# An end stage re-balanced: crossed halves evicted by ScalarE, two stores a chunk, a sixth image convolved again, two more buffers

## The chip, the cores and the metric

The kernel runs on one core of one Trainium2 chip. The core has TensorE (PE, matrix products), ScalarE (ACT), VectorE (DVE), GpSimd (POOL) and SyncE (SP); SP issues nearly all loads and the stores to scratch, POOL the stores of the result. 16 DMA engines move the data. The metric is the device time in microseconds (us).

## The reference

The input x is 16 images of 64 channels and 128 x 128 pixels, fp32. Four residual layers follow one another, each on a group norm of x (32 groups of 2 channels):

```
x = x + conv1x1(gram(gn(x)) @ gn(x))                  # layer 0
x = x + |sobel_x(gn(x))| + |sobel_y(gn(x))|           # layer 1
x = x + conv3x3(temporal_shift(gn(x)), W) + b         # layer 2
y = conv1x1(conv3x3(gn(x), w_bin), w1x1) + b1x1       # layer 3
y = batch_norm(y) over all 16 images                  # mean and variance per channel
x = x + clip(leaky(y), 0, 255)
```

The batch norm needs the sums of y over every pixel of every image before a single result can be finished. So layer 3 has a first pass, which makes y and its sums, and an end stage, which normalizes, clips, adds and writes the result.

## The kernel before, in words

**Main pipeline.** An image is cut into NS = 8 chunks of 2 x 8 rows: partitions 0 to 63 hold 64 channels of the upper half of the image, partitions 64 to 127 those of the lower half. A loop over steps (lines 1176 to 1242) lets three stages, Front (layers 0 and 1), Layer2 and Layer3, work on different images in the same step; `starts` (line 1091) holds their offsets. Every instruction goes through `InOrder`, so each engine runs its instructions in the order in which the Python code emits them. Layer 2 writes its result, the input of layer 3, to a scratch tensor `x3_d` (`put_rows`, line 817), layer 3 its y to `y_d` (line 1059). In the profile both the layer-1 and the layer-2 scratch tensors are called `x_d`.

**Two kinds of images.** For images in `AGAIN` (line 24: 3, 4, 5, 6, 7), y is summed but not stored (line 1059), their x3 is stored in upper and lower halves (`in_halves`, line 819) and their norm coefficients are kept (line 894). In the end stage their chunks are *convolved again*: x3 is loaded, normed, and convolved with the combined weights. For the other images y and x3 are only *loaded*.

**The end stage's list.** Lines 1113 to 1121 write out the order: `todo` holds an entry "again" for every chunk of an image in AGAIN, and an entry "loaded" for every eighth of another image. It starts with two "again" and eight "loaded" (`ahead`), ends with six "loaded" (`behind`), and spreads the others evenly between the "again" entries.

**Buffers and loads.** `room` is a queue of free buffers of 128 x 1024 fp32 (0.5 MB). `fetch` (line 1146) takes the next entry of `todo`, takes one buffer ("again") or two ("loaded") from the front of `room` and issues the loads on SP. Buffers are what the main pipeline no longer needs: from line 1212 on pieces of xw and xh and the tiles x, xr, u and e, at the last image v2, d2[1], q2 and x3, and after the loop (lines 1245 and 1246) the last x3 and y. Loads are issued in the last steps already, as far as room goes. In the end loop `fetch` runs while more than 8 buffers lie in `room` (line 1355).

**The end loop** (lines 1335 to 1358). For "again": `again_close` lets ACT norm the row below the chunk that came before, and `again_products` emits that chunk's matmuls. For "loaded": ACT takes a relu with the batch norm's scale and shift in place, DVE clips and adds, POOL stores 0.5 MB; then `again_out` finishes the chunk convolved before the newest one, and `again_in` lets ACT norm the newest chunk into `v_again`. `again_products` (line 1299) works on 64 x 64 quarters of the array: output row groups g = 0, 1 and input halves h = 0, 1 give four products at a time into `two_again`, whose group g = 0 has the halves in place and whose group g = 1 has them crossed: half h lies in the partitions of half 1 - h. So the residual rows of g = 1 are moved across too, by two products with the identity into `rest_again`, in PSUM. `again_out` (line 1319) then evicts each group by one ACT instruction into z, DVE clips and adds, and POOL stores each group's two halves: four stores of 128 KB a chunk.

The tiles `two` (tag "two") and the v3 tiles have two buffers each, z has one per group.

Of the kernel before, what the change touches and what calls it, by code (L numbers as in the profile page):

```python
# [10 lines left out]
F32 = mybir.dt.float32  # L11
AF = mybir.ActivationFunctionType
ALU = mybir.AluOpType
AX = mybir.AxisListType

B, C, H, W = 16, 64, 128, 128
P = 128
# [3 lines left out]
R = 8  # L21
NS = HH // R
EARLY = 3
AGAIN = (3, 4, 5, 6, 7)
CP = 4
GN_EPS = 1e-5
BN_EPS = 1e-5
# [83 lines left out]
def tile_kernel(ctx: ExitStack, tc: tile.TileContext, x, cw_h, w2_t, b2, wbin_t, w1_t, b1, gamma, beta, consts, out):  # L111
    nc = tc.nc
    pe, dve, act, sp, pool = (InOrder(tc, e) for e in (nc.tensor, nc.vector, nc.scalar, nc.sync, nc.gpsimd))
# [8 lines left out]
    def k(name):  # L122
        return kc[:, AT[name][0]:AT[name][1]]

    def const(shape, name):
        return cpool.tile(shape, F32, name=name)
# [3 lines left out]
    gamma_sb, beta_sb = (const([P, 2], n) for n in ("gamma_sb", "beta_sb"))  # L130
    kept = const([P, len(AGAIN), 2], "kept")
    bn_sum = cpool.tile([P, B * NS], F32, name="bn_sum")
# [7 lines left out]
    def flat(ap):  # L140
        return ap.rearrange("p j w -> p (j w)")

    def halves(d, h, r0, n):

        v = d[0:C * HW].rearrange("(c r) -> c r", r=HW)
        return v[:, (h * HH + r0) * W:(h * HH + r0 + n) * W]
# [15 lines left out]
    ps_one = ctx.enter_context(tc.tile_pool(name="ps_one", bufs=1, space=PSUM))  # L162
    ps_po = ctx.enter_context(tc.tile_pool(name="ps_po", bufs=1, space=PSUM))
# [6 lines left out]
    def cols(o):  # L170
        return slice(o * C, (o + 1) * C)
# [53 lines left out]
    d2, q2, d3 = [], None, None  # L225
    for name in ("d2a", "d2b", "q2", "d3"):
        t = wpool.tile([P, 2, CP, W + 2], F32, name=name)
# [5 lines left out]
        else:  # L233
            d3 = t
# [319 lines left out]
    lo, hi = slice(0, C), slice(C, P)  # L554
# [262 lines left out]
    def put_rows(b, s, j, t):  # L817

        in_halves = b in AGAIN
        size = NP // 2 if in_halves else NP  # L820
# [15 lines left out]
    class Layer2:  # L836
# [49 lines left out]
        def done(self, co):  # L886
# [5 lines left out]
            coefs3[self.b] = co, edge  # L892
            if self.b in AGAIN:
                pool.tensor_copy(kept[:, AGAIN.index(self.b)], co[:, 0:2])

# [101 lines left out]
    class Layer3:  # L997
# [34 lines left out]
        def at(self, i, q):  # L1032
# [10 lines left out]
            if q == 1:  # L1043
# [13 lines left out]
                if 1 <= i:  # L1057
                    y = self.y.pop(i - 1)
                    for s in range(0 if b in AGAIN else 2):
                        for z in range(2):  # L1060
# [42 lines left out]
    at = 12  # L1103
# [8 lines left out]
    N = R * W  # L1112
    parts = deque((b, q) for b in range(B) if b not in AGAIN for q in range(C * HW // P // N))
    again = deque((b, i) for b in AGAIN for i in range(NS))
# [19 lines left out]
    def rest(pool, tag, shape, bufs, n=None):  # L1134
        for m in range(bufs if n is None else n):
            t = pool.tile([P] + shape, F32, tag=tag, name=f"end_{tag}_{len(room)}", bufs=bufs)
            while len(t.shape) > 2:
                t = t.rearrange("p a b c -> p (a b) c" if len(t.shape) == 4 else "p a b -> p (a b)")
            room.append(t[:, 0:N])

    def slices(t, n):
        room.extend(t[:, j * N:(j + 1) * N] for j in range(n))
# [3 lines left out]
    def fetch():  # L1146
        n = fetched[0]
        if n == len(todo):
            return 2
        way, b, q = todo[n]  # L1150
        if way == "loaded":
            yt, rt = room.popleft(), room.popleft()
            sp.dma_start(yt, whole(y_d[b], q))
            sp.dma_start(rt, whole(x3_d[b], q))
            loaded.append((yt, rt))
        else:
            t = room.popleft()
            sp.dma_start(t, x3_d[b].rearrange("(p n) -> p n", p=P)[:, q * N:(q + 1) * N])
            loaded.append((t,))
        fetched[0] += 1  # L1160
        return len(loaded[-1])
# [14 lines left out]
    for step in range(starts[2][1] - 2, steps):  # L1176
        now[0] = step
        for q in range(4):
            for b in range(B):

                i = step - starts[2][1] - NS * b
# [11 lines left out]
            for b in range(1, B):  # L1193
                at, n = pace[b]
# [28 lines left out]
            if step >= last_one and q == 2:  # L1223

                n = 3 if step == last_one else 1 if step < last_one + NS - 2 else 0
# [13 lines left out]
            if step >= last_one - NS and q == 3:  # L1239
                n = 0  # L1240
# [3 lines left out]
        tick()  # L1244
    rest(ring, "x3", [2, CP, W], NS + 2, NS + 2 - 3 - (NS - 3))
    rest(ring, "y", [2, CP, W], 2)
    while len(room) > 1 and fetched[0] < len(todo):
        fetch()

# [12 lines left out]
    def pair(name):  # L1262
        return cpool.tile([P, 2], F32, name=name)
# [13 lines left out]
    sc = pair("sc")  # L1277
# [5 lines left out]
    shb = cpool.tile([P, 1], F32, name="shb")  # L1283
# [15 lines left out]
    def again_products():  # L1299

        v, r, b, i = at_hand[-1]
        two = ps_two.tile([P, 2, CP, W], F32, tag="two", name=f"two_again_{b}_{i}")
        pool_, tag = ((ps_po, "po"), (ps_one, "one"))[(b * NS + i) % 2]
        rest_ = pool_.tile([P, CP, W], F32, tag=tag, name=f"rest_again_{b}_{i}")
        for h in range(2):
            pe.matmul(rest_[cols(1 - h)], k("I")[cols(h), cols(h)], r[cols(h), CP:R, :], start=True, stop=True)
        order = [(ky, kx) for kx in (1, 0, 2) for ky in range(3)]
        for n, (ky, kx) in enumerate(order):
            o0, o1 = (0, W) if kx == 1 else (1, W) if kx == 0 else (0, W - 1)
            for g in range(2):  # L1310
                for h in range(2):
                    j = g * CP + ky
                    pe.matmul(
                        two[cols(h if g == 0 else 1 - h), g, :, o0:o1], rows_of[ky, h][:, kx],
                        v[cols(h), j:j + CP, o0 + kx - 1:o1 + kx - 1], start=n == 0, stop=n + 1 == len(order),
                    )
        summed.append((two, rest_, r, b, i))

    def again_out():

        two, rest_, r, b, i = summed.popleft()
        to = out[b].rearrange("c h w -> (c h w)")
        for g, (tag, add) in enumerate((("c2", r[:, 0:CP, :]), ("c3", rest_))):
            z = ring.tile([P, CP * W], F32, tag=tag, name=f"z_{b}_{i}_{g}", bufs=1)
            act.activation(z, flat(two[:, g]), AF.Relu, bias=shb, scale=sc[:, 1:2])
            to_rows = flat(r[:, g * CP:(g + 1) * CP, :])
            dve.scalar_tensor_tensor(to_rows, z, 255.0, flat(add), op0=ALU.min, op1=ALU.add)
            for h in range(2):
                pool.dma_start(halves(to, h if g == 0 else 1 - h, i * R + g * CP, CP), to_rows[cols(h)])
        room.append(flat(r))  # L1330

    rows_of = {(kk, i): w3[cols(i), slot, :, cols(o)] for slot, i, o, kk in TO_PAIRS}
    summed, coming = deque(), deque()

    for n, (way, b, q) in enumerate(todo):
        if way == "again":
            (t,) = loaded.popleft()
            if n > 0:
                again_close(t)
                again_products()  # L1340
                coming.append((b, q, t))
        else:
            yt, rt = loaded.popleft()
            act.activation(yt, yt, AF.Relu, bias=sh[:, 0:1], scale=sc[:, 0:1])
            dve.scalar_tensor_tensor(rt, yt, 255.0, rt, op0=ALU.min, op1=ALU.add)
            pool.dma_start(whole(out[b].rearrange("c h w -> (c h w)"), q), rt)
            room.extend((yt, rt))
            if len(summed) > 1 or summed and n > len(todo) - behind + 1:
                again_out()
            if coming:  # L1350
                again_in(*coming.popleft())
            elif n == len(todo) - behind + 1:
                again_close(None)
                again_products()
        while len(room) > 8 and fetched[0] < len(todo):
            fetch()
    while summed:
        again_out()
# [38 lines left out]
```

## Time and profile before

| | |
|---|---|
| median of 3 runs | 2587.8 us (2585.97 to 2590.42) |
| the profiled execution | 2585.35 us, its span 2583.5 us |
| PE busy over the span | 2421.9 us (94%) |
| DVE, ACT busy | 2086.3 (81%), 2075.6 (80%) |
| POOL busy | 539.8 (21%) |
| moved by DMA | 613.29 MB, 237 GB/s on the mean |

The stages, from the busy times by stage:

| window, us | what | PE busy | DVE | ACT | POOL | GB/s |
|---|---|---|---|---|---|---|
| 200 to 2111 | the pipeline, three stages at once | 1874.83 | 1752.65 | 1657.59 | 344.27 | 205 |
| 2111 to 2174 | layer 3 of the last image alone | 59.59 | 20.75 | 48.40 | 0.00 | 220 |
| 2174 to 2583.5 | the end stage | 359.53 | 158.95 | 241.28 | 132.94 | 403 |

A busy time is the sum of an engine's instructions, overlap counted once. GB/s is what all DMA engines moved in the window. A line in order of time begins with start and length in us, then names engine, operation, and the tile written and the tile read. "SPq" is SP's queue of DMA issues; its length is the time that the issues span, not the transfer. Two 64 x 64 matmuls that run side by side are recorded each, and an fp32 matmul is recorded twice, so the 36 products of a chunk convolved again are 72 records (2880 for 40 chunks).

### The profile page before, as it was taken

What the parts mean: (1) busy time and instruction counts of PE and PEld (TensorE: products, weight loads), DVE (VectorE), ACT (ScalarE), POOL (GpSimd) and SP (SyncE); (2) the same over time, 40 slices, a digit from 0 to 9 for tenths busy, and PEclk for the clock granted to TensorE, in tenths of its full rate; (3) what the DMA queues carried; (4) which work ended last, traced back from release to release, by engine and by line L of the source; (5) the groups of instructions that cost most, each with busy time, mean ns of one, the idle gap of its engine ahead of it and who ended that gap; (6) DMA issues with size and microseconds to landing.
All of it is one profiled execution on the core that took longest, in us unless ns stands there. A gap on an engine that the chain in (4) does not pass through costs nothing.

```text
span 2583.5 us, 52173 instructions
## 1 busy us (share of the span) xinstructions
PE 2421.9 (94%) x18790; PEld 959.1 (37%) x18790; DVE 2086.3 (81%) x2803; ACT 2075.6 (80%) x3467; POOL 539.8 (21%) x876
## 2 busy tenths in 40 slices
PE   6568899999999999999999999999999999999885
PEld 4334343434343434343434343333333333333332
DVE  4998899999999999999999999999996334433333
ACT  4778879898989898989898988888987668655554
POOL 3332312111121212111212121202110101333332
PEclk8679999999999999999999999999999999999998
DMA  8789979898977777777778877877876877999998
GB/s 200 200 231 241 241 178 251 213 247 208 241 190 201 188 193 190 197 193 187 200 199 222 226 191 192 206 198 203 212 194 170 199 208 252 415 417 417 416 415 354
DMA packets 635809, 613.29 MB, mean 237 GB/s; under 512 B 55280, under 2 KB 535312, under 8 KB 635552
## 3 DMA queue, kind: packets, MB, share of 16 engines
q1 hardware_dynamic: 601376, 505.08, 71.2%
q0 software_dynamic: 34176, 104.88, 12.2%
q8 instruction: 149, 2.44, 0.4%
q14 instruction: 108, 0.88, 0.1%
HBM read 325.59 MB, written 247.47 MB: 222 GB/s over the span
## 4 chain that ended last, share of the span: by engine, by line
PE 48%; DMA 19%; DVE 13%; ACT 8%; issue 5%; SPq 5%; POOL 1%; DVEq 0%; POOLq 0%; ACTq 0%
PE two L74 24%; PE one L74 16%; SPq L74 5%; DVE u L74 5%; PE bank L74 3%; PE po L74 3%; DMA xw<-y_d 3%; DVE e L74 2%; DMA x_d<-u 2%; DMA end_x<-x_d 2%; ACT v L74 2%; DMA xw<-x_d 2%; DVE d L74 2%; DMA v<-x_d 2%; DVE y L74 1%
## 5 line engine op out<-in xcount | busy, mean ns | idle before, releaser
L74 PE MATMUL two<-d,w 64*64 64x512 f32 (+2 forms) x2992 | 692.5, 593 | 0.0
L74 PE MATMUL two_again<-v_again,w 64*64 64x508 f32 (+1 forms) x2880 | 357.0, 598 | 20.9 <-ACT v_again L74 20.8
L74 PE MATMUL one<-v,w 128*64 128x508 f32 (+2 forms) x1600 | 358.8, 580 | 8.1 <-ACT c L74 7.8
L74 PEld LDWEIGHTS two<-d,w 64*64 64x64 f32 (+1 forms) x2992 | 206.6, 134 | 418.0 <-issue 408.1
L74 PE MATMUL one<-v,wi 128*64 128x508 f32 (+3 forms) x1536 | 352.5, 593 | 0.0
L74 DVE SCALAR_TENSOR_TENSOR e<-e 128x1032 f32<-128x1032 f32 (+1 forms) x256 | 313.2, 1224 | 0.0
L74 ACT ACTIVATE xh<-po,co 128x128 f32<-128x128 f32 (+1 forms) x480 | 274.5, 621 | 25.5 <-PE po L74 20.5
L74 PE MATMUL po<-x,abd 64*64 64x512 f32 (+1 forms) x1024 | 187.1, 623 | 53.4 <-ACT xh L74 50.0
L74 DVE SCALAR_TENSOR_TENSOR y<-two,c 128x1024 f32<-128x1024 f32 x128 | 156.1, 1220 | 92.5 <-ACT v L74 62.3
L74 POOL DMA_DIRECT2D q<-d2b x138 | 72.1, 527 | 720.5 <-DVE d2b L74 409.7
L74 PE MATMUL two<-q,cross 64*64 64x508 f32 (+3 forms) x944 | 216.6, 573 | 0.0
L74 PEld LDWEIGHTS two_again<-v_again,w 64*64 64x64 f32 x2880 | 135.6, 134 | 211.5 <-issue 169.7
L74 POOL DMA_DIRECT2D q<-d2a x138 | 73.7, 537 | 641.1 <-issue 284.0
L74 ACT ACTIVATE v<-x,co 128x1024 f32<-128x1024 f32 (+3 forms) x256 | 203.8, 847 | 0.0
L74 DVE TENSOR_TENSOR d<-v 128x1024 f32<-128x1024 f32 x128 | 156.2, 1220 | 47.0 <-ACT v L74 29.3
L74 PEld LDWEIGHTS one<-v,w 128*64 128x64 f32 x1600 | 110.0, 136 | 202.8 <-issue 160.5
L74 ACT ACTIVATE v<-v,co 128x1154 f32<-128x1154 f32 x128 | 172.1, 1345 | 16.1 <-DMA x_d<-x 6.6
L74 PE MATMUL two<-d2a,wi 128*64 128x508 f32 (+1 forms) x768 | 183.2, 589 | 0.0
L74 DVE SCALAR_TENSOR_TENSOR u<-xh 128x1170 f32<-128x1170 f32 x128 | 175.9, 1374 | 5.9 <-ACT xh L74 4.7
L74 DVE SCALAR_TENSOR_TENSOR u<-xh,co,u 128x1024 f32<-128x1024 f32 x128 | 163.8, 1280 | 15.7 <-ACT u L74 15.6
L74 PE MATMUL two<-d2b,wi 128*64 128x508 f32 (+3 forms) x768 | 175.2, 567 | 0.0
L74 PEld LDWEIGHTS one<-v,wi 128*64 128x64 f32 x1536 | 101.1, 138 | 193.8 <-issue 154.9
(265 smaller groups left out, 4349.8 us busy)
## 6 DMA issues: line engine op xcount, KB each, us to landing
x<-in_x SPq DMA_DIRECT2D x256, 256.0 KB
x_d<-u SPq DMA_DIRECT2D x512, 128.0 KB
x_d<-x SPq DMA_DIRECT2D x491, 128.0 KB
xr<-in_x SPq DMA_DIRECT2D x120, 512.0 KB
y_d<-y SPq DMA_DIRECT2D x352, 128.0 KB
v<-x_d SPq DMA_DIRECT2D x448, 72.1 KB
v<-x_d SPq DMA_DIRECT2D x224, 144.2 KB
end_x<-x_d SPq DMA_DIRECT2D x42, 512.0 KB
```

Of the source, the lines that this page charges most:

```text
L74: return self.tc.keep_in_program_order(call(*args, **kwargs))
```

## The change

Four edits. (1) `rest_again` and its products with the identity go; ACT's eviction of the crossed group is split into two instructions of 64 partitions, each reading one half of `two_again` and writing the other half of z, so z has its halves in place and DVE adds the residual from the loaded tile. (2) POOL stores each half of a finished chunk, both groups at once: two stores of 256 KB in place of four of 128 KB. (3) Image 8 joins `AGAIN`, so 48 chunks are convolved again and 80 parts are loaded, in place of 40 and 88; its y is not stored in the first pass. (4) After the loop, d2[0] and d3, tiles of layer 3, join `room`, behind the last x3 and y tiles.

```
-AGAIN = (3, 4, 5, 6, 7)
+AGAIN = (3, 4, 5, 6, 7, 8)
...
     rest(ring, "y", [2, CP, W], 2)
+    for t in (d2[0], d3):
+        slices(t.rearrange("p n j w -> p (n j w)"), 1)
     while len(room) > 1 and fetched[0] < len(todo):
         fetch()
...
         two = ps_two.tile([P, 2, CP, W], F32, tag="two", name=f"two_again_{b}_{i}")
-        pool_, tag = ((ps_po, "po"), (ps_one, "one"))[(b * NS + i) % 2]
-        rest_ = pool_.tile([P, CP, W], F32, tag=tag, name=f"rest_again_{b}_{i}")
-        for h in range(2):
-            pe.matmul(rest_[cols(1 - h)], k("I")[cols(h), cols(h)], r[cols(h), CP:R, :], start=True, stop=True)
...
-        summed.append((two, rest_, r, b, i))
+        summed.append((two, r, b, i))
...
-        two, rest_, r, b, i = summed.popleft()
+        two, r, b, i = summed.popleft()
         to = out[b].rearrange("c h w -> (c h w)")
-        for g, (tag, add) in enumerate((("c2", r[:, 0:CP, :]), ("c3", rest_))):
+        for g, tag in enumerate(("c2", "c3")):
             z = ring.tile([P, CP * W], F32, tag=tag, name=f"z_{b}_{i}_{g}", bufs=1)
-            act.activation(z, flat(two[:, g]), AF.Relu, bias=shb, scale=sc[:, 1:2])
+            for o, at in ((slice(0, P), slice(0, P)),) if g == 0 else ((lo, hi), (hi, lo)):
+                act.activation(z[o], flat(two[at, g]), AF.Relu, bias=shb[at], scale=sc[at, 1:2])
             to_rows = flat(r[:, g * CP:(g + 1) * CP, :])
-            dve.scalar_tensor_tensor(to_rows, z, 255.0, flat(add), op0=ALU.min, op1=ALU.add)
-            for h in range(2):
-                pool.dma_start(halves(to, h if g == 0 else 1 - h, i * R + g * CP, CP), to_rows[cols(h)])
+            dve.scalar_tensor_tensor(to_rows, z, 255.0, to_rows, op0=ALU.min, op1=ALU.add)
+        for h in range(2):
+            pool.dma_start(halves(to, h, i * R, R), flat(r)[cols(h)])
         room.append(flat(r))
```

## The prediction

> **What bounds the kernel now.** I read the page's slices first, then busy time by stage, then the chain of waits, and last the order of instructions on TensorE (PE), ScalarE (ACT) and SyncE's queue (SP) inside the last stage. Busy time by stage (columns: window, length, then busy us of PE, weight loads, VectorE (DVE), ACT, GpSimd (POOL), granted clock, DMA share, GB/s):
>
> ```profile
> 2176.00:2186.00 10.00, 10.00 (x86) 3.52 (x80) 7.39 (x11) 9.29 (x9) 2.67 (x5) 0.87 0.94 322
> 2240.00:2290.00 50.00, 50.00 (x448) 19.77 (x442) 19.68 (x21) 29.76 (x37) 18.26 (x34) 1.00 1.03 417
> 2340.00:2550.00 210.00, 188.06 (x1590) 72.35 (x1584) 75.45 (x83) 121.15 (x150) 65.55 (x123) 1.00 1.03 416
> ```
>
> The DMA engines move 416 to 417 GB/s in both later windows, so they are full from about 2186 us. PE is full too in the second window, but not in the third. The chain of waits agrees: through the stage it goes from load to load down to 2500 us, such as (start, us)
>
> ```profile
> 2198.12 19.30 DMA end_x<-x_d
> 2217.49 19.93 DMA xw<-y_d
> ```
>
> So bytes set the end; PE comes close behind. Its own pace is seen early, while loads done ahead last. One chunk and the start of the next in order of time (start, us):
>
> ```profile
> 2210.94 0.59 PE L74 MATMUL rest_again<-end_x,kc 64*64 64x512 f32 x2
> ...
> 2211.37 0.60 PE L74 MATMUL rest_again<-end_x,kc 64*64 64x512 f32 x2
> 2211.44 8.28 PE L74 MATMUL two_again<-v_again,w 64*64 64x512 f32 x70
> 2219.48 0.60 PE L74 MATMUL rest_again<-end_x,kc 64*64 64x512 f32 x2
> ```
>
> A chunk that is convolved at the end costs PE 8.54 us (2219.48 - 2210.94) with no gap. The two starts of `rest_again` are 0.43 us apart, and a chunk is 20 such slots: 18 for the convolution's 72 recorded matmuls, four quarters of the array at once, and 2 for the copy by the identity. From 2338.65 to 2549.93 the same starts come 10.06 us apart (211.28 / 21): there the loads are late.
>
> **Part by part.**
>
> *Bytes at the end.* A unit is 128x1024 fp32, 0.524 MB. A part that is only loaded moves three (y and x3 in, the result out), a chunk convolved again two. Before: 88 x 3 + 40 x 2 = 344 units. After: 80 x 3 + 48 x 2 = 336. Eight units are 4.19 MB, at 416 GB/s 10.1 us, all on the path. A rule of the Trainium skill disagrees on the price: "DMA: Bandwidth & Descriptors", section Specifications, puts the HBM limit of a core at about 358 GB/s, which would make it 11.7 us (an estimate from that page). The row decides: 416, with one core running. I take -10.1.
>
> *Two more buffers.* The SP queue at the turn into the stage:
>
> ```profile
> 2158.18 16.25 SPq L74 DMA_DIRECT2D y_d<-y  x12
> ...
> 2177.93 0.32 SPq L74 DMA_DIRECT2D end_y<-x_d  x1
> 2179.24 0.32 SPq L74 DMA_DIRECT2D xw<-x_d  x1
> 2187.80 0.32 SPq L74 DMA_DIRECT2D xw<-y_d  x1
> ```
>
> SP stands behind the last y stores until 2174.4, then issues what room is left, and from 2179.2 waits 8.5 us for a buffer. d2[0] and d3 are last read before 2171, so their two loads go out behind end_y, about 2178.5, ahead of that wait. In the first window above DMA did 322 GB/s: (416 - 322) x 10 us = 0.94 MB unused, against 1.05 MB of new loads. Filled wholly that is 0.94 MB / 416 = 2.3 us; not at all, 0. I take -1.6, nearer the full end, since nothing else is queued there. Queued behind them on SP is only the load that waits until 2187.8 anyway.
>
> *PE.* Per chunk the copy's two slots go: 8.54 - 0.85 = 7.69 us. In sum 40 x 8.54 = 342 us become 48 x 7.69 = 369 us; more work, so it must be asked whether PE becomes the bound. The third chunk starts at 2193.85 now; after, two copies sooner, about 2192.1. Then 46 x 7.69 = 353.7 us: PE could be done at 2546. It is done at 2568.0 now. Bytes between two chunks: 2 + 3 x 66/46 = 6.3 units, 3.30 MB, 7.93 us at 416 (before 2 + 3 x 74/38 = 7.84 units, 9.9 us). So DMA at 7.93 and PE at 7.69 run almost level; of 38 buffers some 20 units (25 us of DMA) are still loaded ahead after the first ten entries, and at 0.24 us a chunk only 11 us of them are eaten. PE costs 0 while it keeps 7.69. From what pace it would set the end stands with the rivals.
>
> *ACT.* The half whose partitions are crossed is evicted in two instructions of 64 partitions. The trace of before has no such eviction from PSUM; the nearest row is `COPY d2a<-d 64x512`, 617 ns mean, half of them into the other 64 partitions, and the 128x512 `z`, 763 ns recorded, 0.67 from start to start. So +0.67 us a chunk. The Trainium skill, "ScalarE: Activation LUTs", section What ACT_TABLE_LOAD costs, speaks against the split: every instruction pays about 280 ns, and 93 ns for a second pointer operand, before its 0.833 ns for each of 512 elements, so 0.80 us (estimate). ACT per chunk by rows: three z 2.0, v 0.39 + 1.13, closing row 0.39, 1.43 relu of 1.13 = 5.5 us; with the rule's 0.80 for the added one 5.7. Both lie under 7.69. What is queued behind it in order:
>
> ```profile
> 2245.33 1.44 ACT L74 ACTIVATE z<-two_again,shb,sc 128x512 f32<-128x512 f32 x2 [2.50 <-PE two_again L74]
> 2246.66 0.49 ACT L74 ACTIVATE v_again<-end_x,kept 128x128 f32<-128x128 f32 x1
> 2247.05 1.23 ACT L74 ACTIVATE v_again<-end_u,kept 128x1024 f32<-128x1024 f32 x1
> 2248.18 1.23 ACT L74 ACTIVATE xw<-xw,sh,sc 128x1024 f32<-128x1024 f32 x1
> 2249.31 0.48 ACT L74 ACTIVATE v_again<-q,kept 128x128 f32<-128x128 f32 x1
> ```
>
> The last row, done at 2249.8, is what PE's next chunk (2253.65) needs: 3.9 us to spare. The third z takes 0.67 of it and the faster PE 0.85; 2.3 remain. Cost 0; without that cover up to 0.67 x 48 = 32 us.
>
> *VectorE* adds from SBUF (686 ns) in place of PSUM (682): 0. Its PE waits for `rest_again` (10.2 us in the third window) go, but the load then waits at the v rows: 0.
>
> *Stores.* Per chunk two of 256 KB for four of 128 KB: POOL issues 80 + 96 = 176 for 88 + 160 = 248, at 0.53 us each. POOL waits for VectorE and loads, so that saves nothing. The packets of the stage are already 4.1 KB on the mean (128.98 MB in 31388 packets over the tiny ones, 2240 to 2550), so size gives 0. The first half's store now leaves 0.7 us later: 0, but for the last chunk.
>
> *Image 8 earlier.* Its y is no longer stored (32 DMAs, 4.2 MB), its x3 is split into halves (a few more DMAs on SP). Images 3 to 7 already do so. First y of images 7, 8 and 9:
>
> ```profile
> 1190.83 1.22 DVE L74 SCALAR_TENSOR_TENSOR y<-two,c 128x1024 f32<-128x1024 f32 x1
> ...
> 1314.68 1.22 DVE L74 SCALAR_TENSOR_TENSOR y<-two,c 128x1024 f32<-128x1024 f32 x1
> ...
> 1438.51 1.22 DVE L74 SCALAR_TENSOR_TENSOR y<-two,c 128x1024 f32<-128x1024 f32 x1
> ```
>
> 123.85 us without the store, 123.83 with it: 0. The sixth `kept` copy and two 32 KB edge loads are off the path: 0.
>
> *Two streams almost level* will sometimes wait for each other, and DMA then idles: +1.3, from 0 up to 6 (0.13 us a chunk).
>
> Sum: -10.1 - 1.6 + 1.3 = -10.4. On the profiled execution, 2585.35 (span 2583.5 and 1.85 around it), that is 2574.95, a span of 2573.1; the median of the runs, 2587.8, lies 2.45 above that execution, so 2577.4.
>
> **The rivals.**
> 1. *PE or ACT sets the end partly.* After the last matmul some 12.5 us must follow (z 2.0, two adds 1.4, a store's issue and landing about 9). So PE at pace p ends the span at 2192.1 + 46p + 12.5. At 7.69 that is 2558; it meets my 2573.1 at p = 8.0. At 8.1 the span is 2577.2 and the time 2581.5. For: 98% use leaves little. Against: the gapless rows above.
> 2. *Slower.* The gap of the late window, 10.06 - 8.54 = 1.52 us a chunk, is not lateness of loads but the way through ACT to PE, and stays with each of 48 chunks: p = 9.21, span 2628, time 2632.6. The point is p = 8.23: from 0.54 us of gap (or a clock of 0.934) it is slower than before. Against: from 2202 to 2288 no gap with the same chain and the clock at 1.00. The gaps began when loads ran out.
> 3. *The bytes bring nothing.* SP keeps about eight loads in flight (19 us each, one every 2.4). If that, or waits of loads for buffers, lowers DMA from 416 to 406 GB/s in the stage (10 us of 390), the cut is eaten: 2587. Against: 416 throughout, with 4-way stores.
>
> **How the numbers follow.** The time is 2577.4 with 0.70; rival 1 at 2581.5 with 0.14; rival 3 at 2587 with 0.08; slower with 0.08. What this measurement tells from no change is about 0.2%, 5 us, so "faster" is under 2582.6: 0.70 + 0.14 and a little of rival 3 above it, 0.85; same 0.07; slower 0.08. The range: below, all of the early loads and no mutual waiting (2587.8 - 12.4 = 2575.4) and up to 5 us from a shorter drain after the last load, now 17 us below full rate: 2570. Above, rival 1 at p = 8.15 (2583.8), so 2584.
>
> **What would show it.** Right: DMA still at 415 or more until some 11 us sooner; no `rest_again`; chunks start about 7.7 us apart from the third on, and PE done between 2546 and 2558; the z of the second half as two rows of 64x512 near 0.65 us each; SP issuing two loads more before its 8.5 us wait; images 7 to 9 as far apart as now. Wrong: starts over 8.2 us apart, ACT waiting for nothing before its z, DMA falling under 410, or z of 64 partitions well above 0.8 us.

## The result, and the profile after

The changed kernel takes 2579.28 us (median of 5 runs, 2574.45 to 2580.69) against 2587.8 us (2585.97 to 2590.42, 5 runs): a ratio of 0.9965, 95% interval 0.9954 to 0.9976. It is faster by 8.5 us; 2577.4 was predicted. A second series of the same kernel, e0 below, gave 0.9968 (0.9955 to 0.9980). The two profiled executions lie less far apart, 2585.35 and 2579.28 us (spans 2583.5 and 2577.4). The 6.1 us between them, where the sum said 10.4, are the first thing to explain.

Busy time by stage of the kernel after, in the windows shown before (columns as there: PE, weight loads, DVE, ACT, POOL, granted clock, DMA share, GB/s):

```profile
2176.00:2186.00 10.00, 8.64 (x80) 2.81 (x72) 7.35 (x12) 9.06 (x9) 2.44 (x5) 1.00 0.94 306
2240.00:2290.00 50.00, 50.00 (x472) 17.40 (x468) 20.57 (x23) 38.49 (x49) 11.92 (x23) 1.00 1.03 411
2340.00:2550.00 210.00, 203.17 (x1892) 79.21 (x1884) 80.89 (x90) 160.43 (x202) 49.13 (x91) 1.00 1.03 415
```

DMA stays nearly as full as before (411 and 415 GB/s; 417 and 416 before). PE now fills 97% of the third window (90% before), ACT 76% (58%), POOL a quarter less. The chain that ended last goes from load to load as before, here down to 2548 us, in the same row form (start, us):

```profile
2345.38 16.54 DMA end_x<-x_d
2361.99 17.40 DMA end_x<-x_d
```

One chunk and the start of the next on ACT, in order of time:

```profile
2248.09 2.37 ACT L74 ACTIVATE z<-two_again,shb,sc 128x512 f32<-128x512 f32 x3 [2.15 <-PE two_again L74]
2250.48 0.49 ACT L74 ACTIVATE v_again<-xh,kept 128x128 f32<-128x128 f32 x1
...
2252.39 1.23 ACT L74 ACTIVATE end_u<-end_u,sh,sc 128x1024 f32<-128x1024 f32 x1
2255.77 1.58 ACT L74 ACTIVATE z<-two_again,shb,sc 128x512 f32<-128x512 f32 x2 [2.15 <-PE two_again L74]
```

Chunks start 7.68 us apart (2255.77 - 2248.09), and ACT stands idle for 2.15 us before both these z, waiting for PE; where a chunk brings it two relus, it is 0.6 to 1.0 us. This pace holds from 2194 to 2448 us. Then chunks come unevenly, and at last with gaps on PE, for instance this one, ahead of which ACT waited for a load of y:

```profile
2548.23 1.24 ACT L74 ACTIVATE q<-q,sh,sc 128x1024 f32<-128x1024 f32 x1 [3.67 <-DMA q<-y_d]
...
2550.34 8.44 PE L74 MATMUL two_again<-v_again,w 64*64 64x512 f32 x52 [5.36 <-ACT v_again L74]
```

The loads done ahead are used up by then, and PE waits through ACT for loads, as in the third window of before.

**Where the profile's missing 4 us are.** I cut each span in three: up to the stage's first `two_again` matmul, from there to the last packet of result data, and what follows that packet. Before: 2173.94 + 406.07 + 3.47. After: 2174.16 + 396.08 + 7.18. The stage gave 9.99 us, and 3.71 came back behind it. The closing windows show it. Before:

```profile
2578.00:2580.00 2.00, 0.00 (x0) 0.00 (x0) 0.00 (x0) 0.00 (x0) 0.00 (x0) 0.50 0.67 270
2580.00:2583.50 3.50, 0.00 (x0) 0.00 (x0) 0.00 (x0) 0.00 (x0) 0.00 (x0) 0.50 0.00 0
```

After:

```profile
2569.00:2571.00 2.00, 0.00 (x0) 0.00 (x0) 0.00 (x0) 0.00 (x0) 0.00 (x0) 0.50 0.51 205
2571.00:2577.40 6.40, 0.00 (x0) 0.00 (x0) 0.00 (x0) 0.00 (x0) 0.00 (x0) 0.50 0.00 0
```

In the second row of each no engine is busy and no byte moves. What runs there is not counted as busy and stands in the line `with tile.TileContext(nc) as tc:`, that is, it is run when the program's context closes: a DRAIN on POOL's sequencer. In each of the thirteen profiles it ends only after the last packet of POOL's own stores. Its row, and that of SP's DRAIN (duration in ns, min/median/max, then first and last start), before:

```profile
L1393 POOLq DRAIN  x3: 46/93/5448, 2577.3 to 2583.2; - x3
L1393 SPq DRAIN  x3: 7/7/7, 2580.7 to 2583.0; - x3
```

After, with POOL's last store in order of time:

```profile
L1392 POOLq DRAIN  x3: 40/93/9056, 2567.6 to 2577.2; - x3
L1392 SPq DRAIN  x3: 7/7/7, 2570.9 to 2576.9; - x3
...
2567.63 0.54 POOL L74 DMA_DIRECT2D out<-end_x  x1 [3.04 <-DVE end_x L74]
```

The longest of the three, the first, took 5.45 us before and 9.06 after. It is taken up together with POOL's last store and ends at 2567.60 + 9.06 = 2576.66 us (before: 2582.7), 0.8 us ahead of the span's end, though the last data has landed at 2570.24 and SP has come to its own DRAIN at 2570.9.

### The profile page after: what moved, and what is told of

It reads as the page before. It is cut to its first block, busy times and chain, and to the rows that moved or that the text cites. A ratio compares the mean times of both kernels' runs of the same rounds, so it can differ in the third digit from the quotient of the medians.

```text
span 2577.4 us, 52786 instructions
## 1 busy us (share of the span) xinstructions
PE 2436.5 (95%) x19206; PEld 958.9 (37%) x19206; DVE 2091.8 (81%) x2811; ACT 2137.0 (83%) x3549; POOL 504.3 (20%) x805
## 4 chain that ended last, share of the span: by engine, by line
PE 46%; DMA 20%; DVE 15%; ACT 7%; SPq 7%; issue 4%; POOL 1%; DVEq 0%; POOLq 0%; ACTq 0%
PE two L74 22%; PE one L74 15%; SPq L74 7%; DVE u L74 5%; DMA end_x<-x_d 4%; PE bank L74 3%; DVE e L74 3%; PE po L74 2%; DMA x_d<-u 2%; PE two_again L74 2%; DMA x<-in_x 2%; DMA xw<-x_d 2%; ACT v L74 2%; DVE d L74 2%; DVE y L74 2%
## 5 line engine op out<-in xcount | busy, mean ns | idle before, releaser
L74 PE MATMUL two_again<-v_again,w 64*64 64x508 f32 (+1 forms) x3456 | 374.0, 590 | 10.6 <-ACT v_again L74 10.6
L74 ACT ACTIVATE v<-v,co 128x1154 f32<-128x1154 f32 x128 | 172.1, 1344 | 14.0 <-DMA v<-x_d 10.4
```

The costliest lines, as they stand in the source:

```text
L74: return self.tc.keep_in_program_order(call(*args, **kwargs))
```

## The experiments

"Stage" below is the middle part of that cut, "tail" the last. Ratios are to the kernel before on the same chip, with their 95% interval. The start of the stage differed between executions (2171.1 to 2174.8 us), also between kernels that are the same up to there (2173.94 before, 2172.55 in e8); I didn't look into that and compare stages from their own start.

**e1, the sixth image taken out, everything else of the change kept.**

```
-AGAIN = (3, 4, 5, 6, 7, 8)
+AGAIN = (3, 4, 5, 6, 7)
```

> The change without image 8: five images convolved again, crossed eviction, two stores a chunk, two more buffers. Theory (the bytes at the end set the time): bytes as before, so PE's relief of 0.85 us a chunk buys nothing; only the early loads count, up to 2.3 us: time about 2586, last result data near 2579. Rival (PE's relief is what made the gain): about 2580, as with the whole change.

Ratio 1.0003 (0.9993 to 1.0012), 2589.59 us; stage 405.80 against 406.07. Busy time by stage:

```profile
2240.00:2490.00 250.00, 217.68 (x1816) 76.39 (x1806) 89.01 (x99) 167.58 (x203) 53.93 (x100) 0.99 1.03 417
```

PE has 13% free and DMA is at 417 GB/s. The copy's removal, the merged stores and the two buffers are worth nothing while the bytes stay: the stage's whole gain comes with the sixth image. The stage lasts 405.8 to 406.1 us in the three kernels with five images (before, e1, e8) and 394.6 to 396.6 in the eight with six images and no copy. (The tail of e1 is already the long one, 6.90 us.)

**e4, the sixth image and the buffers, but the old `again_products` and `again_out`** (copy by the identity, one eviction a group, four stores):

```
-AGAIN = (3, 4, 5, 6, 7)
+AGAIN = (3, 4, 5, 6, 7, 8)
...
+    for t in (d2[0], d3):
+        slices(t.rearrange("p n j w -> p (n j w)"), 1)
```

(against the kernel before)

> Six images and two more buffers, but the crossed rows copied by the identity, one eviction a group and four stores, as before. Theory (DMA and PE level at 7.9 and 7.7 us a chunk, PE the bound if the copy stays): chunks 8.54 us apart to the end, PE done at 2193.85 + 46 x 8.54 = 2587, span 2599, time about 2603, slower than before. Rival (bytes alone set the time): 2579 as with the whole change.

Slower: ratio 1.0053 (1.0040 to 1.0067), 2602.83 us. Two chunk starts, and busy time by stage:

```profile
2305.74 0.60 PE L74 MATMUL rest_again<-end_v,kc 64*64 64x512 f32 x2
...
2314.28 0.59 PE L74 MATMUL rest_again<-d2a,kc 64*64 64x512 f32 x2
```

```profile
2190.00:2500.00 310.00, 310.00 (x2768) 122.84 (x2764) 115.20 (x128) 186.45 (x246) 107.43 (x202) 1.00 1.03 415
2500.00:2580.00 80.00, 80.00 (x714) 31.62 (x710) 30.81 (x34) 48.91 (x64) 27.32 (x52) 1.00 0.76 287
```

PE runs without a gap at 8.54 us a chunk to the end, and DMA falls to 287 GB/s before it: PE has become the bound. The sixth image needs the copy's removal: without it the same cut in bytes makes the kernel slower.

**e5, a seventh image.**

```
-AGAIN = (3, 4, 5, 6, 7, 8)
+AGAIN = (3, 4, 5, 6, 7, 8, 9)
```

> The whole change with a seventh image, 9, convolved again (56 chunks, 72 loaded parts). Theory (PE is the bound as soon as a chunk's bytes take less than its 7.69 us; here 2 + 3 x 58/54 = 5.2 units, 6.6 us): chunks 7.69 us apart throughout, PE done at about 2190 + 54 x 7.69 = 2605, 12 us to the last data, 5 to 7 of closing: time about 2625. Rival (bytes set the time): another 10 us less, about 2568.

Slower: 1.0162 (1.0148 to 1.0176), 2627.92 us.

```profile
2190.00:2500.00 310.00, 310.00 (x2900) 107.81 (x2896) 108.24 (x125) 228.26 (x297) 67.83 (x125) 1.00 1.00 386
2500.00:2600.00 100.00, 100.00 (x944) 34.81 (x940) 35.16 (x40) 73.10 (x95) 21.69 (x40) 1.00 0.74 265
```

PE is at 100% in both windows, DMA at 386 and 265 GB/s. Between six images (bytes are the bound) and seven (PE) the two limits cross.

**e2, without the two buffers.**

```
-    for t in (d2[0], d3):
-        slices(t.rearrange("p n j w -> p (n j w)"), 1)
```

> The whole change without the two further buffers. Theory as predicted (early loads worth 1.6 us): time about 2581. Rival (the slices after the turn show 306 GB/s with the two loads against 322 before, so nothing was filled): the same as the whole change, 2579.

Ratio 0.9953 (0.9940 to 0.9965), 2576.73 us; stage 396.59 against 396.08 and 395.35 with them (after, e0). SP's queue at the turn, with the buffers (after):

```profile
2178.46 0.32 SPq L74 DMA_DIRECT2D d2a<-x_d  x1
2178.84 0.50 SPq L74 DMA_DIRECT2D d<-x_d  x1
2179.46 0.35 SPq L74 DMA_DIRECT2D xw<-y_d  x1
2188.88 0.99 SPq L74 DMA_DIRECT2D xw<-x_d  x2
```

And without (e2):

```profile
2175.52 0.32 SPq L74 DMA_DIRECT2D end_y<-y_d  x1
2177.01 8.43 SPq L74 DMA_DIRECT2D xw<-x_d  x2
```

The two loads do go out ahead of the long wait. Without them the stage is 0.5 to 1.2 us longer here, and 0.8 shorter in e9 against e3 below: nothing that profiles or times can tell from none.

**e6, the crossed group evicted by one instruction of 128 partitions.** The halves stay crossed, so that it adds and stores them in the wrong rows; its time is that of the change without the split.

```
-            for o, at in ((slice(0, P), slice(0, P)),) if g == 0 else ((lo, hi), (hi, lo)):
+            for o, at in ((slice(0, P), slice(0, P)),):
```

> The whole change, but each group evicted by one instruction of 128 partitions, so that the crossed group's halves stay crossed and are added to the wrong rows. Theory (ScalarE's third eviction, 0.77 us a chunk, is hidden behind PE): as with the whole change within 1 us from the stage's start to the last data. Rival (its 48 x 0.77 = 37 us is on the path in part, as in the late 40 us, where chunks come unevenly): 3 to 10 us less.

Ratio 0.9964 (0.9951 to 0.9976), stage 395.07. Busy time from 2190 to 2460, after:

```profile
2190.00:2460.00 270.00, 270.00 (x2532) 94.01 (x2528) 110.90 (x123) 214.26 (x272) 65.72 (x121) 1.00 1.03 414
```

e6:

```profile
2190.00:2460.00 270.00, 270.00 (x2536) 93.89 (x2528) 109.48 (x121) 177.95 (x234) 65.56 (x121) 1.00 1.03 417
```

ACT is busy for 36 us less, and PE for the same 270: the split is hidden whole.

**e7, the change with four stores of 128 KB a chunk.**

```
             dve.scalar_tensor_tensor(to_rows, z, 255.0, to_rows, op0=ALU.min, op1=ALU.add)
-        for h in range(2):
-            pool.dma_start(halves(to, h, i * R, R), flat(r)[cols(h)])
+            for h in range(2):
+                pool.dma_start(halves(to, h, i * R + g * CP, CP), to_rows[cols(h)])
```

> The whole change but with four stores of 128 KB a chunk, each group as soon as its rows are added; the crossed eviction stays, so the rows lie in place. Theory (fewer, larger stores make the drain longer: 5.45 and 7.32 us in the two profiles with four): drain 5 to 7.5 us, time 2 us less than with two stores, about 2576. Rival (stores' number plays no part): drain and time as with the whole change.

**e0, the change itself again**, on the same chip as e6, e7 and e8.

> The whole change once more, unchanged, beside the next three on one chip: a second profile of it. Theory (GpSimd's closing drain is longer with this change, as in three profiles with two stores a chunk: 9.06, 8.40, 9.05 us against 5.45 before): drain 8 to 9.5 us, the span 6 to 7.5 us past the last result data, time about 2578. Rival (the drain's length is chance from one execution to the next): anything from 5 to 11 us.

e7: ratio 0.9966 (0.9954 to 0.9979), stage 394.70, tail 4.97. e0: 0.9968, stage 395.35, tail 7.20. Merging the stores gains nothing in the stage. In these profiles it goes with a longer drain, 7.01 us in e7 and 9.05 in e0; the 2.2 us of tail between them don't show in the two ratios, whose intervals are 6.5 us wide.

**e3, the closing stores on SP.** The stores at the list's end, of the last five "loaded" entries and of the last two chunks, move from POOL's queue to SP's, whose loads are all issued by then.

```
+    closing = [False]
...
-            pool.dma_start(halves(to, h, i * R, R), flat(r)[cols(h)])
+            (sp if closing[0] else pool).dma_start(halves(to, h, i * R, R), flat(r)[cols(h)])
...
-            pool.dma_start(whole(out[b].rearrange("c h w -> (c h w)"), q), rt)
+            closing[0] = n > len(todo) - behind
+            (sp if closing[0] else pool).dma_start(whole(out[b].rearrange("c h w -> (c h w)"), q), rt)
```

> The whole change, but the stores of the last entries of the list (those behind the last chunk convolved again) go out on SP's queue, not on GpSimd's. Theory (after the last result data, GpSimd's closing drain, 9.06 us long in the change's profile and 5.45 before, is a tail of its own that begins at its last store): GpSimd is drained early, the span ends about 1 us after the last data, time near 2573. Rival (the tail is the program's end and waits for all data whatever the queue): 2579, span 6 to 7 us past the last data.

**e8, the same edit in the kernel before.**

> The kernel before, its last stores on SP's queue as in the run with the closing stores moved. Theory (the drain costs whatever of it lies past the last data, 2.7 us in the profile of before): 2 to 3 us less than before, about 2585.5, against 6 us less in the changed kernel. Rival (SP's queue itself is the faster way to land the last stores, the drain plays no part): the same 5 to 6 us less as in the changed kernel.

e3: ratio 0.9942 (0.9929 to 0.9956), 2573.27 us; stage 395.40, tail 1.58. POOL's drain and the last, empty window of e3:

```profile
L1394 POOLq DRAIN  x3: 40/102/10813, 2544.4 to 2568.5; - x3
```

```profile
2567.20:2568.70 1.50, 0.00 (x0) 0.00 (x0) 0.00 (x0) 0.00 (x0) 0.00 (x0) 0.50 0.00 0
```

The drain is no shorter (10.81 us) but now starts at 2544 us, beside the stage's own work. The last data is followed by 1.5 us instead of 7. e8: ratio 0.9990 (0.9982 to 0.9998), stage 406.13 as before (406.07), tail 1.53 against 3.47, POOL's drain moved likewise:

```profile
L1395 POOLq DRAIN  x3: 40/102/9938, 2554.9 to 2580.0; - x3
```

The stage stays the same in both, so SP's stores don't land sooner: it is the drain alone.

**e9, e3 without the two buffers, and e10, e3 with e7's four stores.**

> The whole change with the closing stores on SP's queue and without the two further buffers. Theory (closing stores worth about 5 us, buffers about nothing): 5 us less than the whole change, within 1 us of the run with the buffers and the closing stores moved, about 2572 to 2573. Rival (the buffers are worth their 1.6 us once the drain doesn't cover it): 2 us slower than with them.

> The whole change with four stores a chunk and the closing stores on SP's queue. Theory (with the drain out of the way the number of stores plays no part): as with two stores, about 2573. Rival (four smaller, earlier stores are themselves better, 0.7 to 1.4 us from the stage's start to the last data in their profile): about 2572.

e9: 0.9942 (0.9930 to 0.9954), stage 394.58, tail 1.59. e10: 0.9957 (0.9945 to 0.9970), stage 396.16, tail 1.37. The buffers change nothing there either, and four stores are no better than two. Over all versions with six images and no copy, the three with closing stores on SP have a mean ratio of 0.9947, the five without (after, e0, e2, e6, e7) 0.9963: 4.2 us, where the profiles' tails differ by some 5.2. Single ratios don't settle it (e2 and e3, on one chip, have intervals that overlap), but the two groups and e8, whose interval lies just under 1, point the same way as the profiles. The lowest ratio of all, 0.9942, is that of e3 and e9.

## Why the prediction was right

*Bytes.* Predicted -10.1 of a sum of -10.4, and the stage is shorter by 9.99 (after) and 10.72 (e0); its last data lands at 2570.24 us instead of 2580.01. The sum itself held for the stage. e1 shows that it is the sixth image. The queue of the loads and of the stores to scratch moved 8.3 MB less over the whole span (496.8 for 505.1 MB): 4.2 MB are the y that is no longer stored, the rest the loads that the sum counts. The trace's 416 was the right price: the kernel after moves 415 GB/s over 210 us, and the 358 GB/s of the Trainium skill ("DMA: Bandwidth & Descriptors", Specifications) did not bind a core that runs alone.

*PE.* The 7.69 us a chunk is what the trace has. Rival 1, PE partly setting the end, didn't show with six images: the last store follows an add on DVE that waits for a load, not for PE.

```profile
2566.10 1.23 DVE L74 SCALAR_TENSOR_TENSOR end_x<-end_x,end_x 128x1024 f32<-128x1024 f32 x1 [2.38 <-DMA end_x<-x_d]
```

No run made PE faster with six images, so this rests on that wait, on DMA's rate and on the size of the gain. That PE was near is shown by e4 (8.54 us: 2602.83) and e5 (seven images), in both of which PE sets the end. Wrong was how long the lead would last: I had 25 us of early loads of which 11 would be eaten, but it ran out around chunk 35 (chunk 40 in e0), and PE was done at 2558.8, past the end of my 2546 to 2558. Whether the lead was shorter or was eaten faster isn't settled. It cost nothing that the stage shows: the bytes ahead of a late load are counted in the sum already.

*Two more buffers.* Mis-sized: -1.6 predicted, between -1.2 and +0.8 measured (e2 against after and e0, e9 against e3). The order of issues was as foretold, but DMA in the first window moved 306 GB/s, not more than the 322 of before, so the 0.94 MB of slack was not filled. What keeps it so low there I didn't find out. As the mutual waiting (+1.3) wasn't measured by itself, it stays a guess that these two errors cancel.

*ACT.* The split costs 36 us of ACT over 270 us and nothing in the end (e6). Its size was low. One eviction of 64 partitions takes

```profile
L74 ACT ACTIVATE z<-two_again,shb,sc x144: 757/774/778, 2189.0 to 2560.4; 64x512 f32<-64x512 f32 x96, 128x512 f32<-128x512 f32 x48
```

0.77 us, the same as one of 128 partitions and close to the 0.80 estimated from the Trainium skill ("ScalarE: Activation LUTs", What ACT_TABLE_LOAD costs). But 36 us over the 35 chunks of that window are 1.03 us a chunk, and I took 0.67. That was the distance between two starts before (two z in 1.44 us), where each overlaps the next by 0.1 us in the record; the z of 64 partitions don't (three in 2.37, starts 0.80 and 0.79 us apart). Why they don't is open. The time to spare comes out accordingly. In a chunk like that of the prediction, with a relu ahead of the closing row:

```profile
2259.69 1.23 ACT L74 ACTIVATE end_v<-end_v,sh,sc 128x1024 f32<-128x1024 f32 x1
2260.82 0.48 ACT L74 ACTIVATE v_again<-xw,kept 128x128 f32<-128x128 f32 x1
...
2263.45 0.78 ACT L74 ACTIVATE z<-two_again,shb,sc 128x512 f32<-128x512 f32 x1 [1.02 <-PE two_again L74]
```

The closing row is done at 2261.30, and PE's next chunk starts 0.2 us before that z, at 2263.24: 1.9 us, where 2.3 were foretold.

*Stores: 0* in the stage, right (e7 against e0: 394.70 and 395.35). *Image 8 earlier: 0*, right, by the first y of images 7, 8 and 9, 123.92 and 123.89 us apart:

```profile
1191.00 1.22 DVE L74 SCALAR_TENSOR_TENSOR y<-two,c 128x1024 f32<-128x1024 f32 x1
...
1314.92 1.22 DVE L74 SCALAR_TENSOR_TENSOR y<-two,c 128x1024 f32<-128x1024 f32 x1
...
1438.81 1.22 DVE L74 SCALAR_TENSOR_TENSOR y<-two,c 128x1024 f32<-128x1024 f32 x1
```

*What no step had.* I reckoned with up to 5 us less from the last full rate of DMA to the end (in the prediction: "a shorter drain after the last load"), and took the end of the span for the end of the data. From the last full rate to the last data it is 14 us in both profiles (2566 to 2580 before, 2556 to 2570 after), no shorter. Behind that lies POOL's own DRAIN, 5.45 us in the profile of before and readable there, and 9.06 after. The tail grew by 3.7 us in the profile, the difference between 10.4 and 6.1 but for the 0.4 by which the stage missed the sum and 0.2 at its start. That it is the drain is shown by e3 and e8, which move it and shorten the tail, with the stage as it was. In the medians the miss is smaller, 1.9 us (2579.28 for 2577.4): the profile of before lay 2.45 under its median, that of after on it, and single runs scatter by more than that. So the closeness of the median is in part luck: the sum had no term for the tail.

*The slower rival* had each chunk keep the late gap of 1.52 us. The early chunks, at 7.68 us with the same chain, show that the gap is lateness of loads.

## What to carry to other kernels

Where a stage is bound by bytes and another engine comes close behind, work out both paces per unit of work, before and after a trade of bytes for arithmetic: here six images at 7.69 us against 7.93 us of bytes pay, while seven, or six at 8.54, lose. An edit that only relieves the engine behind (e1: 1.0003) is worth nothing alone, and can still be what makes the trade possible (e4). Look at what lies between the last byte and the end of the span, and see whether the closing stores can go out on a queue whose end costs less there: 1.4 to 1.6 us here on SP, 3.5 to 7.2 on POOL.

## What the runs showed of the hardware

POOL's closing DRAIN lasts for longer than its stores are on their way. In the kernel after, the data ends at 2570.24 us and the drain at 2576.66. It repeats well: 9.05 to 9.06 us in four profiles (after, e0, e2, e6). Where it stands at the end, it took 5.45 to 7.32 us in the kernels with four stores of 128 KB a chunk (before, e4, e7) and 8.40 to 9.71 in those with two of 256 KB (after, e0, e1, e2, e5, e6). Where it begins inside the stage it took 9.68 to 10.81 (e3, e8, e9, e10). Counted from the last packet of POOL's own queue, it goes on for 2.1 to 4.2 us in the five kernels with four stores a chunk and for 4.4 to 6.5 in the eight with two. What sets its length is not settled. With the closing stores on SP, the end of the span follows the last data by 1.4 to 1.6 us in all four kernels that have them there.

An eviction of 64 partitions by ACT, crossing to the other half of the partitions on its way from PSUM, is recorded as long as one of 128 that doesn't cross (0.77 us). In line it costs more: 0.79 to 0.80 us from start to start, against 0.67 to 0.68 for two of 128 (before, e6). Crossing and half width weren't separated.
